# A cross-attention kernel on one core: the order of the first 60 microseconds and of the last ten

## The chip, the cores and the metric

The kernel runs on one core of a Trainium2 chip. The metric is the device time of one launch in microseconds (us). The time before is 1426.85 us, the median of three runs (1426.43 to 1427.44).

## The reference

64 batches, all in float32; x is 64x256x512, the context c is 64x256x384.

```python
text_p  = einsum('bld,dh->blh', H_l, W_text)  + b_text     # q, 512 wide
audio_p = einsum('bsd,dh->bsh', H_a, W_audio) + b_audio    # k and V, 512 wide
Q = layer_norm(text_p, g1, beta1)
K = layer_norm(audio_p, g2, beta2)
alpha = softmax(einsum('blh,bsh->bls', Q, K) * scale)
H_hyper = einsum('bls,bsh->blh', alpha, audio_p)
H_hyper = einsum('blh,hk->blk', H_hyper, W_out) + b_out
out = layer_norm(H_hyper + H_l, g_out, beta_out)
```

## The kernel before

All is in one function, `tile_xattn_kernel`, with the order of the instructions on every engine written out by hand: each engine runs its instructions in the order of the text, and waits at the first one whose inputs, or whose buffer, are not there yet. The same holds of the queue in which SyncE issues the DMAs.

A batch passes these stages. Its x and c are read as "squares" (`load_x`, `load_c`: four DMAs each, by L88), so that VectorE's transposes of 32x32 blocks (`turn_x`, `turn_c`, L91) give x and c with the channels on the partitions. TensorE multiplies them with the weights; from batch 1 on the two halves of each side are multiplied as seven products instead of eight (class `Blocks`). For these, GpSimd forms sums and differences of the blocks (`sum_x`, `sum_c`, `weight_sums`) and VectorE adds the products from PSUM to the rows that they belong to (`leave`, L483, seven instructions). ScalarE (ACT) takes the squares of the rows (`square`, L380); GpSimd makes the scales of them, (variance + eps) to the power -0.5 (L341, L343); ACT multiplies the rows by these (`normalise`, L408). The rows go to DRAM (`store`, L418) and come back as squares (`fetch`, L88), VectorE turns them (`turn`), ACT applies gamma and beta (`affine`, L446), and then come the scores (L511), maxima (L521), exponentials (L528), and the context (L577). Only batch 0 is different: its c and x come as rows and are transposed on TensorE (`RowTurn`), and its products are whole (`Projection.multiply`, L362), with their moments taken on VectorE.

The weights are centred over the hidden channels first (`means` on ACT, L275; `centre` on VectorE, L282), so that the mean of each later row is zero. W_audio times W_out is formed once (`turn_weights`, `fold_multiply`, `fold_evict`, L245 and L254), with its bias (`bias_parts`, L231 and L233; `fold_bias`), since alpha times V times W_out is alpha times c times that product. `keep_busy` multiplies a tile of ones, with no use of the result. `take_columns` transposes the vectors gamma, beta and b_audio on TensorE and copies them on ACT.

The first part, up to the loop, does all this for batch 0 and the projections of batch 1. Turn b of the loop, for b from 0 to 61, takes the scores of batch b, q and k of batch b + 2, the turn of the squares of batch b + 3, and the output of batch b - 1, among others. Before, the turns and sums of batch b + 3 stand right ahead of the maxima in every turn. After the loop a part written out by hand finishes the last batches: `last` is batch 61, `at` batch 62 and `end` batch 63. The very last rows are multiplied and settled in two halves (`multiply_halves`, `evict_halves`, `settle_halves`), each with a DMA of its own.

`shift` subtracts the mean and multiplies by g_out; `settle` multiplies by the row's scale, which comes from GpSimd (`scales`), and adds beta_out. PSUM has six banks for products and two for the rest; SBUF's work tiles have two buffers each, so a tile of batch b + 2 waits until that of batch b has been read.

Of the kernel before, what the change touches and what calls it, by code (L numbers as in the profile page):

```python
# [15 lines left out]
P = 128  # L16
# [6 lines left out]
def kernel(  # L23
# [82 lines left out]
    def load_squares(b):  # L106
        load_c(b)
        load_x(b)
# [23 lines left out]
    def row(v, name):  # L132
        t = const.tile([P, H], F32, tag=name, name=name)
        nc.sync.dma_start(t, v.rearrange("(o h) -> o h", o=1).broadcast_to([P, H]))
        return t
# [11 lines left out]
    def weight_chunks(t, w, lo, n, queues):  # L147
        v = w.rearrange("(q k i) h -> q i k h", q=NQ, i=SQ)
        for q in range(NQ):
            queues[q].dma_start(t[q * SQ : (q + 1) * SQ, lo : lo + n], v[q, :, lo : lo + n])  # L150

    nc.sync.dma_start(c_0[:, :1], c_rows[:, :1])
    weight_chunks(wa_sb, w_audio, 0, 1, [nc.scalar, nc.sync, nc.scalar, nc.sync])
    nc.scalar.dma_start(c_0[:, 1:], c_rows[:, 1:])
    weight_chunks(wa_sb, w_audio, 1, 2, [nc.sync] * NQ)
    for t in range(LT):
        nc.sync.dma_start(x_0[:, t, :], x_rows[:, t, :])
    weight_chunks(wt_sb, w_text, 0, 2, [nc.sync] * NQ)
# [30 lines left out]
    def keep_busy(n):  # L189

        ps = p_pj.tile([P, P], F32, tag="pj", name="ps_ones")
        for _ in range(n):
            nc.tensor.matmul(ps, lhsT=ones, rhs=ones, start=True, stop=True)  # L193
# [59 lines left out]
    def fold_evict(a):  # L253
        nc.scalar.copy(wao_sb[:, a, :], ps_wao.pop(a))  # L254
# [9 lines left out]
    def moments(mv, src, t):  # L264

        st = small.tile([P, 6], F32, tag="st", name="st")
        nc.vector.bn_stats(st, src)
        nc.vector.bn_aggr(mv[:, t, :], st)

    def means(rows, n, name):  # L270

        m = const.tile([P, n], F32, tag=name, name=name)
        for k in range(n):
            junk = work.tile([P, H], F32, tag="junk", name="junk")
            nc.scalar.activation(  # L275
                junk, rows[:, k, :], AF.Identity, scale=-1.0 / H, accum_out=m[:, k : k + 1]
            )
        return m

    def centre(rows, m, n):  # L280
        for k in range(n):
            nc.vector.tensor_scalar(rows[:, k, :], rows[:, k, :], m[:, k : k + 1], None, ALU.add)  # L282
# [31 lines left out]
    def sum_c(cT, tag="csum"):  # L314

        part = lambda i, j: cT[:, j, bass.ts(i, P)]
        s = work.tile([P, 5, P], F32, tag=tag, name=tag)
        add = nc.gpsimd.tensor_tensor
        add(s[:, 0], part(1, 0), part(1, 1), ALU.add)
        add(s[:, 1], s[:, 0], part(0, 0), ALU.subtract)  # L320
        add(s[:, 2:4], cT[:, 0:3:2, :P], cT[:, 0:3:2, P:], ALU.subtract)
        add(s[:, 4], part(0, 1), s[:, 1], ALU.subtract)
        return {
            1: [part(0, 0)], 2: [part(0, 1), part(0, 2)], 4: [part(1, 1), part(1, 2)],
            5: [s[:, 0], part(1, 2)], 6: [s[:, 1]], 7: [s[:, 2]], 3: [s[:, 4], s[:, 3]],
        }
# [172 lines left out]
    class Attention:  # L499
# [143 lines left out]
            self.r = getattr(self, "r", {})  # L643
            self.r.update({lo + t: r for t, r in enumerate(rstd_of(self.mv[:, lo : lo + n, 1], n))})

        def moments(self):
            self.mv = small.tile([P, LT, 2], F32, tag="mvy", name="mvy")
            for t in range(LT):
                moments(self.mv, self.y[:, t, :], t)
            self.scales()  # L650

        def multiply_halves(self, t):
            self.ps_h = []
# [67 lines left out]
    def turn_c(b):  # L721
        cT = work.tile([P, AC, S], F32, tag="cT", name=f"cT_{b}")
        turn(cT, blocks[b][0], AC)
        return cT

    def add_bias(b):
        xb = rows[b][0]
        for t in range(LT):
            nc.gpsimd.tensor_tensor(xb[:, t, :], xb[:, t, :], bao_sb, ALU.add)  # L729
# [6 lines left out]
    x_turn = RowTurn(x_0, DC, "xT")  # L736
    k[0] = Projection("k", 0, c_turn.T, wa_sb, ba_sb, AC, ST)
    q[0] = Projection("q", 0, x_turn.T, wt_sb, bt_sb, DC, LT)
    keep_busy(12)
    c_turn.tile(0)  # L740
    keep_busy(8)
    k[0].multiply(0, [0])
    c_turn.tile(1)
    k[0].multiply(1, [0])
    k[0].multiply(0, [1, 2])
    k[0].multiply(1, [1, 2])
    mean_wa = means(wa_sb, AC, "mwa")
    war = []
    for a in range(AC):
        war.append(work.tile([P, HC, P], F32, tag="e" if a == 0 else "eT", name=f"war_{a}"))  # L750
        arrange(war[a], wa_sb[:, a, :], HC, nc.gpsimd.tensor_copy)
    x_turn.tile(0)
    x_turn.tile(1)
    centre(wa_sb, mean_wa, AC)
    wa_blocks = weights_of_three(wa_sb, "wasum")
    for chunks in ([0, 1], [2, 3]):
# [1 line left out]
            q[0].multiply(t, chunks)  # L758
    ba_row = ba_sb.rearrange("p (o h) -> p o h", o=1)
    bt_row = bt_sb.rearrange("p (o h) -> p o h", o=1)  # L760
    k[0].evict(0)
    k[0].evict(1)
    k[0].scales()
    mean_ba = means(ba_row, 1, "mba")
    mean_wt = means(wt_sb, DC, "mwt")
    cT[1] = turn_c(1)
    cs = {1: sum_c(cT[1])}
    centre(ba_row, mean_ba, 1)
    k[0].normalise()
    k[0].store()  # L770
    load_vectors()
    k[0].fetch()
    centre(wt_sb, mean_wt, DC)
    waT = turn_weights()
    wt_blocks = weight_sums(wt_sb, DC // 2, "wtsum")
    q[0].evict(0)
    q[0].evict(1)
# [2 lines left out]
    centre(bt_row, mean_bt, 1)  # L780
    q[0].normalise()
    q[0].store()
    bo_sb = row(b_out, "bo")
    q[0].fetch()
    load_squares(2)
    xT[1] = turn_x(1)
    k[1] = Blocks("k", 1, cs.pop(1), wa_blocks, ba_sb)
    k[1].products(1, 2)
# [6 lines left out]
    k[1].leave(3)  # L795
    k[1].leave(7)
    k[1].products(4)
    g1_sb, be1_sb, g2_sb, be2_sb, bac_sb = take_columns()
    k[1].leave(4)
    k[1].square()  # L800
    k[1].scales()
    xs = {1: sum_x(xT[1])}

    for v in (g2_sb, be2_sb):
        nc.vector.tensor_scalar(v, v, scale, None, ALU.mult)
    k[0].turn()
    k[1].normalise()
    k[1].store()
    k[1].fetch()
    k[0].affine(g2_sb, be2_sb)  # L810
    load_squares(3)
    fold_multiply(0)
    fold_evict(0)
    fold_multiply(1)
    fold_evict(1)
    part = bias_parts()
    xT[2] = turn_x(2)
    xs[2] = sum_x(xT[2])
    cT[2] = turn_c(2)
    cs[2] = sum_c(cT[2])  # L820
    q[0].turn()
    q[0].affine(g1_sb, be1_sb)
    q[1] = Blocks("q", 1, xs.pop(1), wt_blocks, bt_sb)
    q[1].products(1, 2)
    q[1].leave(1)
    q[1].products(6, 5)
    q[1].leave(6)
    q[1].leave(2)
# [5 lines left out]
    q[1].leave(4)  # L834
    q[1].square()
    q[1].scales()
    fold_multiply(2)
    fold_evict(2)
    bao_sb = fold_bias(part)
# [8 lines left out]
    for b in range(B - 2):  # L848
        three = b + 3 < B
        at = Attention(b)  # L850
        at.scores()
        if done:
            done.o.leave(3)
            done.o.leave(7)
            done.o.leave(4)
            done.add_x()
        if last:
            last.turn_e()
        if three:
            xT[b + 3] = turn_x(b + 3)  # L860
            xs[b + 3] = sum_x(xT.pop(b + 3))
            cT[b + 3] = turn_c(b + 3)
            cs[b + 3] = sum_c(cT.pop(b + 3))
        at.maxima()
        at.exponentials()
        q2 = q[b + 2] = Blocks("q", b + 2, xs.pop(b + 2), wt_blocks, bt_sb)
        q2.products(1, 2)
        q2.leave(1)
        at.reciprocals()
        at.divide_e()  # L870
        if b:
            q[b + 1].fetch()
            k[b + 1].fetch()
        at.store_e()
        if b + 4 < B:
            load_squares(b + 4)
        at.fetch_e()
        rows[b + 1] = load_rows(b + 1)
        if done:
            done.statistics()  # L880
        q2.products(6, 5)
        q2.leave(6)
        q2.leave(2)
        q2.leave(5)
        q2.products(7, 3)
        q2.leave(3)
        q2.leave(7)
        q2.products(4)
        q2.leave(4)
        q2.square()  # L890
        q2.scales()
        q[b + 1].turn()
        if done:
            done.shift(0)
            done.shift(1)
        if last:
            last.context()
        q[b + 1].affine(g1_sb, be1_sb)
        k[b + 1].turn()
        k[b + 1].affine(g2_sb, be2_sb)  # L900
        if done:
            done.settle(0)
            done.settle(1)
            done.store()
        q2.normalise()
        q2.store()
        if last:
            last.start_products()
        k2 = k[b + 2] = Blocks("k", b + 2, cs.pop(b + 2), wa_blocks, ba_sb)
        k2.products(1, 2)  # L910
        k2.leave(1)
        k2.products(6, 5)
        k2.leave(6)
        k2.leave(2)
        k2.leave(5)
        k2.products(7, 3)
        k2.leave(3)
        k2.leave(7)
        k2.products(4)
        k2.leave(4)  # L920
        k2.square()
        k2.scales()
        k2.normalise()
        k2.store()
        if last:
            last.o.products(1, 2)
            last.o.leave(1)
            last.o.products(6, 5)
            last.o.leave(6)
            last.o.leave(2)  # L930
            last.o.leave(5)
            last.o.products(7, 3)
            last.o.products(4)
        done, last = last, at
# [41 lines left out]
    at.context()  # L976
    done.settle(1)
    done.store()
    last.moments()
    end = Attention(B - 1)  # L980
    end.scores(end=True)
    at.start_output()
    at.multiply(0)
    last.shift(0)
    end.maxima()
    end.exponentials()
    last.shift(1)
    last.settle(0)
    last.settle(1)
# [18 lines left out]
    end.scales(0, 1)  # L1008
    end.multiply_halves(1)
    end.shift(0)  # L1010
    end.settle(0)
    end.store(0, 1)
    end.evict_halves(1)
    end.scales(1, 1)
    end.shift(1)
    end.settle_halves(1)


# [30 lines left out]
```

## Time and profile before

| | us |
|---|---|
| median of three runs | 1426.85 |
| the profiled execution, own time | 1425.56 |
| its span, first to last instruction | 1423.7 |
| TensorE busy | 1407.9 |
| VectorE busy | 1272.0 |
| ACT busy | 932.1 |
| GpSimd busy | 874.3 |

The busy shares of the whole span come first, and the chain of work that ended last, followed back from the last instruction. In a timeline each line has the start and the length of a group of instructions, the engine (PE is TensorE, DVE is VectorE, POOL is GpSimd, SPq is SyncE's DMA queue), the line of the kernel, the operation with its tiles, and how many there are; in brackets stands how long the engine had stood idle before it, and what ended that. Starts are microseconds from the first instruction. A float32 matmul shows as two records. Where a group shows no bracket, the engine went straight on.

The granted clock of TensorE is 0.998 over the span. Its activity is dense in all but the first and the last of 40 slices.

### The profile page before, as it was taken

Reading aid. Unit: us, or ns where it says so; the run is one execution under the profiler, and the core shown is the slowest. Engines: PE = TensorE matmul, PEld = TensorE weight load, DVE = VectorE, ACT = ScalarE, POOL = GpSimd, SP = SyncE. Lnnn points to the kernel's source line nnn. Section 1 sums busy time; section 2 is a strip of 40 time slices with the busy share of each in tenths; the row PEclk is TensorE's granted clock in tenths of the full one; section 3 lists DMA queues with packets and bytes.
Section 4 is the critical chain, followed back from the end, with each engine's and each line's share of the span. In section 5 each row is a group of like instructions: output and inputs, shape, how many; then the busy total and the mean of one; then the engine's idle time right before and its main releaser. Section 6 shows DMA issues by size and latency. Waiting matters only on the chain.

```text
span 1423.7 us, 23376 instructions
## 1 busy us (share of the span) xinstructions
PE 1407.9 (99%) x6465; PEld 1223.3 (86%) x6465; DVE 1272.0 (89%) x2134; ACT 932.1 (65%) x2293; POOL 874.3 (61%) x1295
## 2 busy tenths in 40 slices
PE   9899999999999999999999999999999999999997
PEld 6688888888888888888888888888888888888885
DVE  5689999999999999999999999999999999999987
ACT  4566676676766766766766766767767667667662
POOL 5556566566576566666666665665755665666644
PEclk9999999999999999999999999999999999999999
DMA  8798888787888878878878887887888788888763
GB/s 196 190 259 239 239 229 236 226 231 238 234 226 236 241 216 240 246 210 238 238 225 233 234 230 227 235 235 228 227 240 236 219 241 243 215 238 244 206 195 105
DMA packets 450582, 322.61 MB, mean 227 GB/s; under 512 B 154900, under 2 KB 382996, under 8 KB 450452
## 3 DMA queue, kind: packets, MB, share of 16 engines
q1 hardware_dynamic: 450212, 320.78, 80.0%
q8 instruction: 53, 0.87, 0.3%
q14 instruction: 77, 0.63, 0.1%
q10 hardware_dynamic: 240, 0.33, 0.1%
HBM read 204.09 MB, written 116.92 MB: 225 GB/s over the span
## 4 chain that ended last, share of the span: by engine, by line
PE 93%; DVE 2%; POOL 2%; DMA 1%; issue 1%; ACT 1%; SPq 0%; DVEq 0%; POOLq 0%
PE ps_q L472 26%; PE ps_y L472 20%; PE ps_k L472 20%; PE ps_sc L511 15%; PE ps_z L577 11%; PE ps_q L362 1%; PE ps_ones L193 0%; SPq L88 0%; DMA qd<-qr 0%; POOL yr L593 0%; PE ps_k L362 0%; POOL x L729 0%; DVE qr L483 0%; POOL ve L341 0%; POOL rstd L343 0%
## 5 line engine op out<-in xcount | busy, mean ns | idle before, releaser
L511 PE MATMUL ps_sc<-kT,qT 128*128 128x256 f32 x1024 | 232.0, 380 | 3.9 <-ACT kT L446 3.2
L341 POOL TENSOR_SCALAR ve<-var 128x2 f32<-128x2 f32 x126 | 42.9, 341 | 307.2 <-ACT junk L380 307.2
L528 ACT ACTIVATE e<-ps_sc,nmx 128x256 f32<-128x256 f32 x128 | 59.4, 469 | 250.1 <-DVE nmx L521 250.1
L511 PEld LDWEIGHTS ps_sc<-kT,qT 128*128 128x128 f32 x1024 | 193.9, 190 | 32.4 <-ACT kT L446 4.2
L483 DVE TENSOR_TENSOR qr<-ps_q,qr 128x512 f32<-128x512 f32 x378 | 188.3, 512 | 33.9 <-PE ps_q L472 18.2
L483 DVE TENSOR_TENSOR kr<-ps_k,kr 128x512 f32<-128x512 f32 x378 | 188.4, 512 | 24.7 <-PE ps_y L472 0.5
L483 DVE TENSOR_TENSOR yr<-ps_y,yr 128x512 f32<-128x512 f32 x372 | 185.3, 512 | 24.1 <-DVE yr L483 0.9
L593 POOL TENSOR_TENSOR yr<-yr,x 128x512 f32<-128x512 f32 x124 | 156.9, 1275 | 58.1 <-DVE yr L483 58.1
L577 PE MATMUL ps_z<-eT,c 128*128 128x256 f32 x768 | 176.5, 379 | 0.1
L472 PE MATMUL ps_q<-wtsum,xsum 128*128 128x256 f32 x756 | 173.4, 379 | 0.0
L343 POOL TENSOR_TENSOR rstd<-ve,nhalf 128x2 f32<-128x2 f32 (+1 forms) x194 | 158.2, 816 | 16.1
L472 PE MATMUL ps_k<-wa,cT 128*128 128x256 f32 x630 | 166.8, 379 | 0.0
L472 PE MATMUL ps_y<-wao,zT 128*128 128x256 f32 x620 | 164.2, 379 | 0.0
L577 PEld LDWEIGHTS ps_z<-eT,c 128*128 128x128 f32 x768 | 145.8, 190 | 20.7 <-ACT e L528 0.5
L472 PEld LDWEIGHTS ps_q<-wtsum,xsum 128*128 128x128 f32 x756 | 143.6, 190 | 19.5
L380 ACT ACTIVATE junk<-kr 128x512 f32<-128x512 f32 x126 | 79.4, 630 | 97.0 <-DVE kr L483 97.0
L446 ACT ACTIVATE qT<-qT,columns 128x256 f32<-128x256 f32 x256 | 133.0, 592 | 11.5 <-DVE qT L91 11.5
L472 PEld LDWEIGHTS ps_k<-wa,cT 128*128 128x128 f32 x630 | 119.6, 190 | 16.2
L446 ACT ACTIVATE kT<-kT,columns 128x256 f32<-128x256 f32 x256 | 132.3, 590 | 0.7 <-DVE kT L91 0.5
L472 PEld LDWEIGHTS ps_y<-wao,zT 128*128 128x128 f32 x620 | 117.7, 190 | 16.0
L408 ACT ACTIVATE kr<-kr,rstd 128x512 f32<-128x512 f32 x126 | 84.1, 714 | 71.0 <-POOL rstd L343 71.0
L701 DVE SCALAR_TENSOR_TENSOR yr<-yr,rstd,beo 128x512 f32<-128x512 f32 x124 | 126.8, 1060 | 0.0
(150 smaller groups left out, 2950.9 us busy)
## 6 DMA issues: line engine op xcount, KB each, us to landing
kd<-kr SPq DMA_DIRECT2D x64, 512.0 KB, 3.1
kq<-kd SPq DMA_DIRECT2D x256, 128.0 KB, 3.4
qd<-qr SPq DMA_DIRECT2D x64, 512.0 KB, 4.9
qq<-qd SPq DMA_DIRECT2D x256, 128.0 KB, 3.3
xq<-in_x_dram SPq DMA_DIRECT2D x252, 128.0 KB, 2.9
x<-in_x_dram SPq DMA_DIRECT2D x63, 512.0 KB, 4.1
out_dram<-yr SPq DMA_DIRECT2D x62, 512.0 KB, 4.9
cq<-in_ctx_dram SPq DMA_DIRECT2D x252, 96.0 KB, 2.5
```

The lines of the kernel that those rows point to most:

```text
L341: nc.gpsimd.tensor_scalar(ve, var, EPS, None, ALU.add)
L343: nc.gpsimd.tensor_tensor(r, ve, nhalf[:, :n], ALU.pow)
L380: nc.scalar.activation(junk, self.rows[:, t, :], AF.Square, scale=1.0 / math.sqrt(H), accum_out=self.var[:, t : t + 1],)
L408: nc.scalar.mul(row, row, self.r[t])
L446: nc.scalar.activation(self.T[:, k, :], self.T[:, k, :], AF.Identity, bias=bet[:, k : k + 1], scale=gam[:, k : k + 1],)
L472: nc.tensor.matmul(bank[:, j, :], lhsT=side, rhs=w, start=(i == 0), stop=(i == len(pairs) - 1))
L483: add = lambda o, i0, i1: nc.vector.tensor_tensor(o, i0, i1, ALU.add)
L511: nc.tensor.matmul(self.sc[:, t, :], lhsT=self.qT[:, k, bass.ts(t, P)], rhs=self.kT[:, k, :], start=(k == 0), stop=(k == HC - 1),)
L528: nc.scalar.activation(self.e[:, t, :], self.sc[:, t, :], AF.Exp, bias=self.nmx[:, t : t + 1], accum_out=self.den[:, t : t + 1],)
L577: nc.tensor.matmul(ps[:, j, :], lhsT=self.c_sb[:, s, bass.ts(lo + j, P)], rhs=self.eT[:, s, :], start=(s == 0), stop=(s == ST - 1),)
L593: nc.gpsimd.tensor_tensor(self.y[:, t, :], self.y[:, t, :], self.xb[:, t, :], ALU.add)
L701: nc.vector.scalar_tensor_tensor(self.y[:, t, :], self.y[:, t, :], self.r[t], beo_sb, ALU.mult, ALU.add)
```

## The change

At the start: fewer multiplies of ones; the second tile of batch 0's c is issued by SyncE, behind W_audio, instead of ACT; the products of batch 0's k run by tile, not by chunk; ACT takes the means of W_audio after its copies of x; k[0]'s first eviction stands ahead of centring W_audio; k[0]'s scales stand behind the sums of c[1]; centring W_text and turning W_audio stand ahead of normalising k[0]. The squares of batches 2 and 3 are issued one input at a time, behind a fetch or a store, instead of both together behind the fetch. The first two folds stand ahead of the columns and their evictions behind normalising k[1]. The turn of k[0] follows, q[0]'s turn and affine stand behind the first leave of q[1], and batch 2's turns and sums behind q[1]'s scales. In the first turn of the loop batch 3's turns and sums stand behind q[2]'s scales instead of ahead of the maxima; all later turns are as before.

At the end: `moments` can take one tile; the second moments and the first shift of batch 61 stand behind batch 63's maxima and exponentials; the settle and store of batch 63's first rows stand behind the evictions and shift of its last rows.

No computation is added or left out but the multiplies of ones. The diff, with the loop's context cut:

```diff
     weight_chunks(wa_sb, w_audio, 0, 1, [nc.scalar, nc.sync, nc.scalar, nc.sync])
-    nc.scalar.dma_start(c_0[:, 1:], c_rows[:, 1:])
     weight_chunks(wa_sb, w_audio, 1, 2, [nc.sync] * NQ)
+    nc.sync.dma_start(c_0[:, 1:], c_rows[:, 1:])
...
-        def moments(self):
-            self.mv = small.tile([P, LT, 2], F32, tag="mvy", name="mvy")
-            for t in range(LT):
+        def moments(self, tiles=range(LT)):
+            if 0 in tiles:
+                self.mv = small.tile([P, LT, 2], F32, tag="mvy", name="mvy")
+            for t in tiles:
                 moments(self.mv, self.y[:, t, :], t)
-            self.scales()
+            if LT - 1 in tiles:
+                self.scales()
...
+    def turn_next(b):
+        xT[b] = turn_x(b)
+        xs[b] = sum_x(xT.pop(b))
+        cT[b] = turn_c(b)
+        cs[b] = sum_c(cT.pop(b))
...
-    keep_busy(12)
+    keep_busy(6)
     c_turn.tile(0)
-    keep_busy(8)
-    k[0].multiply(0, [0])
+    keep_busy(2)
+    k[0].multiply(0, range(AC))
     c_turn.tile(1)
-    k[0].multiply(1, [0])
-    k[0].multiply(0, [1, 2])
-    k[0].multiply(1, [1, 2])
-    mean_wa = means(wa_sb, AC, "mwa")
+    k[0].multiply(1, range(AC))
     war = []
...
     x_turn.tile(0)
     x_turn.tile(1)
+    mean_wa = means(wa_sb, AC, "mwa")
+    k[0].evict(0)
     centre(wa_sb, mean_wa, AC)
...
-    k[0].evict(0)
     k[0].evict(1)
-    k[0].scales()
     mean_ba = means(ba_row, 1, "mba")
     mean_wt = means(wt_sb, DC, "mwt")
     cT[1] = turn_c(1)
     cs = {1: sum_c(cT[1])}
+    k[0].scales()
     centre(ba_row, mean_ba, 1)
+    centre(wt_sb, mean_wt, DC)
+    waT = turn_weights()
     k[0].normalise()
     k[0].store()
     load_vectors()
     k[0].fetch()
-    centre(wt_sb, mean_wt, DC)
-    waT = turn_weights()
+    load_c(2)
     wt_blocks = weight_sums(wt_sb, DC // 2, "wtsum")
...
     q[0].store()
-    bo_sb = row(b_out, "bo")
+    load_x(2)
     q[0].fetch()
-    load_squares(2)
     xT[1] = turn_x(1)
...
     k[1].products(4)
-    g1_sb, be1_sb, g2_sb, be2_sb, bac_sb = take_columns()
     k[1].leave(4)
     k[1].square()
     k[1].scales()
     xs = {1: sum_x(xT[1])}
+    fold_multiply(0)
+    fold_multiply(1)
+    g1_sb, be1_sb, g2_sb, be2_sb, bac_sb = take_columns()
...
-    k[0].turn()
     k[1].normalise()
     k[1].store()
+    bo_sb = row(b_out, "bo")
+    load_c(3)
     k[1].fetch()
+    load_x(3)
+    fold_evict(0)
+    fold_evict(1)
+    k[0].turn()
     k[0].affine(g2_sb, be2_sb)
-    load_squares(3)
-    fold_multiply(0)
-    fold_evict(0)
-    fold_multiply(1)
-    fold_evict(1)
     part = bias_parts()
-    xT[2] = turn_x(2)
-    xs[2] = sum_x(xT[2])
-    cT[2] = turn_c(2)
-    cs[2] = sum_c(cT[2])
-    q[0].turn()
-    q[0].affine(g1_sb, be1_sb)
     q[1] = Blocks("q", 1, xs.pop(1), wt_blocks, bt_sb)
     q[1].products(1, 2)
     q[1].leave(1)
+    q[0].turn()
+    q[0].affine(g1_sb, be1_sb)
     q[1].products(6, 5)
...
     q[1].scales()
+    xT[2] = turn_x(2)
+    xs[2] = sum_x(xT[2])
+    cT[2] = turn_c(2)
+    cs[2] = sum_c(cT[2])
     fold_multiply(2)
...
-        if three:
-            xT[b + 3] = turn_x(b + 3)
-            xs[b + 3] = sum_x(xT.pop(b + 3))
-            cT[b + 3] = turn_c(b + 3)
-            cs[b + 3] = sum_c(cT.pop(b + 3))
+        if three and b:
+            turn_next(b + 3)
         at.maxima()
         at.exponentials()
...
         q2.scales()
+        if three and not b:
+            turn_next(b + 3)
         q[b + 1].turn()
...
-    last.moments()
+    last.moments([0])
     end = Attention(B - 1)
     end.scores(end=True)
     at.start_output()
     at.multiply(0)
-    last.shift(0)
     end.maxima()
     end.exponentials()
+    last.moments([1])
+    last.shift(0)
     last.shift(1)
...
     end.shift(0)
-    end.settle(0)
-    end.store(0, 1)
     end.evict_halves(1)
     end.scales(1, 1)
     end.shift(1)
+    end.settle(0)
+    end.store(0, 1)
     end.settle_halves(1)
```

## The prediction, made before the changed kernel was run

> **What bounds the kernel now.** I read the page's busy shares and chain first, then the timeline of each engine over the first 95 us and the last 30 us, since those are the only stretches that the change edits. The page:
>
> ```profile
> PE 1407.9 (99%) x6465; PEld 1223.3 (86%) x6465; DVE 1272.0 (89%) x2134; ACT 932.1 (65%) x2293; POOL 874.3 (61%) x1295
> ...
> PE 93%; DVE 2%; POOL 2%; DMA 1%; issue 1%; ACT 1%; SPq 0%; DVEq 0%; POOLq 0%
> ```
>
> TensorE is the bound, and 93% of the chain is its matmuls. Its timeline shows where it is not dense:
>
> ```profile
> 1.53 5.16 PE L193 MATMUL ps_ones<-ones 128*128 128x128 f32 x24 [1.53 <-POOL ones L122]
> 6.86 1.95 PE L193 MATMUL ps_ones<-ones 128*128 128x128 f32 x16
> 10.56 4.56 PE L362 MATMUL ps_k<-wa,cT 128*128 128x512 f32 x10 [0.57 <-ACT cT L210]
> 47.95 3.90 PE L511 MATMUL ps_sc<-kT,qT 128*128 128x256 f32 x16 [0.69 <-ACT qT L446]
> 65.88 3.90 PE L511 MATMUL ps_sc<-kT,qT 128*128 128x256 f32 x16 [3.24 <-ACT kT L446]
> 87.75 3.62 PE L511 MATMUL ps_sc<-kT,qT 128*128 128x256 f32 x16
> ```
>
> Ahead of 10.56 it mostly multiplies ones; at 65.88 (the scores of batch 1) it stands 3.24 us. From there it repeats with no gap, 21.58 us a batch (87.75 to 109.33 and on). So the start is worth what it moves that 65.88; the end is a chain of its own. Why the scores stand, on VectorE and in SyncE's DMA queue:
>
> ```profile
> 44.03 1.25 DVE L91 STREAM_TRANSPOSE xT<-xq 128x1024 f32<-128x1024 f32 x1 [6.11 <-DMA xq<-in_x_dram]
> 45.20 0.93 DVE L91 STREAM_TRANSPOSE cT<-cq 128x768 f32<-128x768 f32 x1
> 46.06 1.20 DVE L91 STREAM_TRANSPOSE qT<-qq 128x1024 f32<-128x1024 f32 x1
> 47.18 0.65 DVE L483 TENSOR_TENSOR qr<-ps_q,bt 128x512 f32<-128x512 f32 x1
> 61.98 1.25 DVE L91 STREAM_TRANSPOSE qT<-qq 128x1024 f32<-128x1024 f32 x1 [1.47 <-DMA qq<-qd]
> ```
>
> ```profile
> 35.45 2.04 SPq L88 DMA_DIRECT2D qq<-qd x4
> 37.53 2.01 SPq L88 DMA_DIRECT2D cq<-in_ctx_dram x4
> 39.58 1.93 SPq L88 DMA_DIRECT2D xq<-in_x_dram x4
> ```
>
> TensorE had q[1]'s first products done at 38.5, but VectorE takes them only at 47.18: it stands 6.11 us for batch 2's squares, which SyncE issues behind qq, and then turns them. The rest of the leaves end at 51.2; square, scale, store and fetch of q[1] end at 61.98, then come the turn and the affine, and the scores at 65.88.
>
> **The change part by part: the first 66 us.** I put the new order of each engine on the old durations.
>
> *Fill-in and first products.* 12 of 20 ones-multiplies go (24 of 40 records). c's second tile moves from ACT's to SyncE's queue, behind 512 KB of w_audio: there 704 KB (256 KB records between the waits at 5.17 and 8.17) took 3.0 us, 235 GB/s, so w_audio lands 0.8 us earlier (7.4) and c's tile about 8.2; x's issues slip by one issue, 0.4, hidden by a queue that is 4.2 behind. TensorE: 12 records at 0.216 from 1.53 end at 4.1; c's first copy ends at 4.4; transposes and four more records to about 5.9; first chunk 5.9 to 6.8 (0.87 each), the others 7.4 to 9.15; second tile's transposes to 9.5, ACT copy 0.48, three products 10.05 to 12.65. Then x's transposes begin, 14.96 before: 2.3 earlier. w_text's first half (2.2 MB cumulative at 235 GB/s from 2 us, so 11.5[...]) is there for q at 13.9. q ends at 21.0 instead of 23.37.
>
> [...] The trace: the ones take 0.216 a record until 5.85, 0.12 after; 4.3 us of activity bring the full rate. [...] The new order leaves a hole of 0.3 us at 4.1. If the hole doesn't matter, nothing is lost; if the 4.3 us start again at 4.45, full rate comes at 8.8 and k's first products take 5.9 to 10.0, 0.85 later. I take the first ([...]the old 0.57 hole at 10.0 cooled nothing) and keep 0.85 for the range.
>
> *GpSimd.* The means of w_audio now follow ACT's copies of x (means 14.3 to 16.1); k's first eviction runs before centring, and w_audio is centred at 16.7 (16.0 before). Second eviction and statistics 1.6, turn of c[1] 0.95: 19.2. On GpSimd the sums of c (2.2) now stand ahead of k's scales (2.0): 23.5 for k's scales, 21.4 before. Weight sums (5.6) and q's scales (1.5) give 30.6, as before (30.7): centring w_text and the weight transposes ahead of k's normalising gain nothing there. ACT: q normalised at 32.1, squares of k[1] 33.7, GpSimd scales 34.7, xsum's first two of x[1] at 36.5 to 37.0.
>
> *TensorE on.* Weight transposes 1.66, k[1]'s products 4.75, two folds 6.9 and the columns' transpose 0.1: 21.0 to 34.4. q[1]'s first pair ends at 36.15; the next pair needs xsum: a new wait of 0.3 to 0.9, 0.6 taken. q[1] ends 41.1, third fold and bias 45.4, scores(0) 45.4 (47.95 before), q[2] 48.85 to 54.9, k[2] to 59.65 (62.64 before).
>
> *VectorE and its waits.* The columns' transpose now lies behind the folds: VectorE is done with k[1]'s leaves at 32.0 and stands to 34.8 for ACT's copy; queued behind are the two column scalings, k[0]'s turn, part and q[1]'s leaves. That costs nothing, since part (3.5) ends at 39.8, and q[1] waits for q[0]'s turn anyway. ACT's fold evictions after k[1]'s normalising (37.1) free banks needed at 41.1.
>
> *SyncE.* K's store waits for ACT: 25.1 (22.61). kq is issued 29.3 to 31.1, load_c(2) 31.1 to 33.1, qd 33.1 (32.27, so the store loses 0.8), load_x(2) to 35.4, qd lands at 36.5, qq to 38.4 and lands near 41.0. So load_c(2) and load_x(2), eight issues at 0.5, lie in two waits for stores; kd[1] goes at 38.4 instead of 41.62; bo, load_c(3), kq[1] and load_x(3) end at 45.8. q[0]'s turn is at 41.0 to 42.2, its affine to 44.3: 1.1 before the scores need it. q[1]'s other leaves end at 45.4 (51.2). Square and scales to 47.0, normalised 48.4, stored 48.5, fetch from 51.8, landed by 56.3.
>
> *Turns.* Batch 2's turns (2.1) lie at 45.4 to 47.5, sums on GpSimd at 47.0 to 52.1, q[2] needs the first two at 50.6. Batch 3's turns and sums, which stood ahead of the maxima at 53.40, now follow q[2]'s leaves: these end with TensorE's last product, 55.6. Then turns 2.1 to 57.7, q[1]'s turn 1.25, k[1]'s turn beside ACT; ACT's q affine 2.06 from 59.1, first k column 0.58: scores(1) at 61.7. TensorE was free at 59.65, so a wait of 2.1 stays and is now set by VectorE. Gain: 65.88 - 61.7 = 4.2. Batch 3's sums (done at 62.5) are needed at 65.2: hidden.
>
> **The end.**
>
> ```profile
> 1414.43 0.75 DVE L696 SCALAR_TENSOR_TENSOR y<-y,mvy,go 128x512 f32<-128x512 f32 x1
> 1415.94 0.75 DVE L701 SCALAR_TENSOR_TENSOR y<-y,rstd,beo 128x512 f32<-128x512 f32 x1 [0.75 <-POOL rstd L343]
> 1420.18 0.88 DVE L684 SCALAR_TENSOR_TENSOR y<-y,rstd,beo 128x256 f32<-128x256 f32 x2 [0.76 <-POOL rstd L343]
> ```
>
> VectorE is the chain here and stands twice for GpSimd's scale. The change moves the first settle (0.67 of step) behind the last shift, into the second wait: the halves follow at 1415.1 (their matmuls end at 1415.1), so 0.76 + 0.67 = 1.4 goes; the last scale then stays 1.55 behind the last moments, as before. The store of the first 256 KB moves to 1418.7, half a microsecond ahead of the halves: the trace moves 256 KB in about 1.0 (1417.4 to 1418.4), so contention costs 0 to 0.3; 0.1 taken. Maxima ahead of the second moments fill a wait of 0.31, but the scale then comes 0.1 late: 0.1 gained; TensorE's 0.48 wait there isn't on the chain. End: 1.4.
>
> **Sum.** 4.2 + 1.4 = 5.6. The profiled execution, span 1423.7 and own time 1425.56, becomes 1418.1 and 1420.0. It lies 1.3 under the median 1426.85 of three; so the median becomes 1421.3.
>
> **Rivals.** *The start gives part:* full rate late (0.85), the w_audio tile no earlier (0.8), xsum's wait 0.9 instead of 0.6: 2.0 less, 1423.3. For it: GpSimd has no slack from 19 to 37. *The start gives almost nothing* because VectorE's new order only trades waits (columns, then qq, then batch 3's turns ahead of q[1]'s): scores(1) within 1 us of now and the end's 1.4: 1425. Against it: each of these ends before the next thing it feeds. *The early qq turns into a block, slower:* q[0]'s turn now stands ahead of six leaves of q[1]. With qq landing at L, q[1]'s turn is ready at L + 15.3 and scores(1) at L + 19.3. It decides from L = 42.4 and loses all above 46.6 (48.0 with the end); at L = 51, as if kq, cq, xq and qd ran one after the other at the 4 us each that a landing took, scores(1) come at 70.3 and the kernel at 1429.9. Against it: in the old trace qq was there by 46.06 at the latest, issued 35.45, and its landing took 2.9.
>
> **Numbers.** As worked out 65%; partly 14%; start lost 13%; slower 8%. The range 1419.5 to 1424.3 holds the first two: 5.6 less 2.6 at most, or with TensorE free at 59.65 and no wait 2 more. 0.2% is 2.85 us, about what a measurement of this kernel can tell from no change: faster (under 1424.0) 0.77, same 0.15, slower 0.08.
>
> **What would show it.** Right: first k products near 6, x's transposes near 12.7, no wait on ACT qT at scores(0), q[1]'s leaves done near 45.4, scores(1) near 61.7 with a wait of about 2 on ACT kT behind turns of batch 3, then 21.58 a batch; the last settle beside GpSimd's scale. Wrong: matmuls at half rate past 6 us; a DMA named as what ended VectorE's idle before qT at 41 or later; any new TensorE gap behind 66 us.

## The result, and the profile after

| | before | after |
|---|---|---|
| median of six runs each, us | 1426.64 (1425.84 to 1427.44) | 1421.76 (1420.36 to 1422.65) |
| profiled execution, own time | 1425.56 | 1420.47 |
| its span | 1423.7 | 1418.7 |
| start of the scores of batch 1 | 65.88 | 61.47 |
| from the scores of batch 63 to the end | 26.8 | 26.1 |

The ratio is 0.9964, with an interval of 0.9951 to 0.9977: 4.9 us faster in the medians, 5.1 in the profiled executions. The last two rows split the 5.1: 4.41 from the start (the scores of batch 63 move by just as much, 1396.95 to 1392.54, so nothing is won or lost in between) and 0.7 from the end. Five of the 14 profiles lose 1.6 to 2.7 us to a fall of TensorE's granted clock, told of below; single spans are compared at the starts of instructions ahead of such a fall.

The page of the changed kernel, its busy shares and its chain:

```profile
PE 1405.0 (99%) x6441; PEld 1220.9 (86%) x6441; DVE 1273.3 (90%) x2134; ACT 931.8 (66%) x2293; POOL 875.2 (62%) x1295
...
PE 94%; DMA 2%; DVE 1%; POOL 1%; SPq 1%; issue 1%; ACT 0%; POOLq 0%; DVEq 0%; ACTq 0%
```

TensorE is the bound as before; its 24 records less are those of ones. Its timeline:

```profile
1.53 2.93 PE L193 MATMUL ps_ones<-ones 128*128 128x128 f32 x12 [1.53 <-POOL ones L122]
...
5.80 3.34 PE L362 MATMUL ps_k<-wa,cT 128*128 128x512 f32 x6
...
12.71 1.04 PE L209 MATMUL ps_rows<-ident,xTr 128*128 128x128 f32 x8
...
45.16 3.62 PE L511 MATMUL ps_sc<-kT,qT 128*128 128x256 f32 x16
...
61.47 3.90 PE L511 MATMUL ps_sc<-kT,qT 128*128 128x256 f32 x16 [1.90 <-ACT kT L446]
...
83.34 3.62 PE L511 MATMUL ps_sc<-kT,qT 128*128 128x256 f32 x16
```

The first products stand at 5.80, the transposes of x 2.2 us earlier than before, and the wait for q's turn at the first scores (0.69) is gone. But the first of the six records was not at full rate (1142 ns, where the last take 592). L362 in parts of this stretch (shortest, median and longest record in ns, then the first and last start):

```profile
L362 PE MATMUL ps_k<-wa,cT x1: 1142/1142/1142, 5.8 to 5.8; 128*128 128x512 f32 x1
...
  DMA wa<-in_L_xattn_W_audio_dram: 0.8, 1
...
L362 PE MATMUL ps_k<-wa,cT x3: 592/592/592, 7.7 to 8.5; 128*128 128x512 f32 x3
```

The second record starts 0.93 behind the first, where the last ones follow each other by 0.43. The loss cost nothing: the weights of the third record could be loaded only when w_audio's next part had landed, at 7.06 (the 0.8 in the middle).

At 61.47 a wait of 1.90 is left of 3.24. Its row names the same releaser as before, but the cause is another, as VectorE shows:

```profile
41.24 1.25 DVE L91 STREAM_TRANSPOSE qT<-qq 128x1024 f32<-128x1024 f32 x1 [0.56 <-DMA qq<-qd]
42.41 3.23 DVE L483 TENSOR_TENSOR qr<-ps_q,qr 128x512 f32<-128x512 f32 x6
45.55 1.24 DVE L91 STREAM_TRANSPOSE xT<-xq 128x1024 f32<-128x1024 f32 x1
...
55.59 1.24 DVE L91 STREAM_TRANSPOSE xT<-xq 128x1024 f32<-128x1024 f32 x1
56.75 0.94 DVE L91 STREAM_TRANSPOSE cT<-cq 128x768 f32<-128x768 f32 x1
57.61 1.20 DVE L91 STREAM_TRANSPOSE qT<-qq 128x1024 f32<-128x1024 f32 x1
```

The 6.11 us for batch 2's squares are gone: q[1]'s leaves end at 45.6 instead of 51.2. The last three rows have no bracket: VectorE goes straight through batch 3's turns into q[1]'s turn, so that turn no longer waits for a DMA but for two turns ahead of it. SyncE's queue:

```profile
33.03 2.45 SPq L88 DMA_DIRECT2D xq<-in_x_dram  x4
35.85 2.29 SPq L88 DMA_DIRECT2D qq<-qd  x4
...
48.89 0.38 SPq L418 DMA_DIRECT2D qd<-qr  x1
51.71 1.79 SPq L88 DMA_DIRECT2D qq<-qd  x4
```

Batch 2's x is now issued ahead of q[0]'s fetch, in the time in which q[0]'s store lands. At the end VectorE has these waits:

```profile
1399.60 1.42 DVE L703 SCALAR_TENSOR_TENSOR yr<-yr,rstd,beo 128x512 f32<-128x512 f32 x2 [0.60 <-POOL rstd L343]
...
1413.23 0.75 DVE L698 SCALAR_TENSOR_TENSOR y<-y,mvy,go 128x512 f32<-128x512 f32 x1
1413.90 0.74 DVE L703 SCALAR_TENSOR_TENSOR y<-y,rstd,beo 128x512 f32<-128x512 f32 x1
1415.11 0.88 DVE L686 SCALAR_TENSOR_TENSOR y<-y,rstd,beo 128x256 f32<-128x256 f32 x2 [0.46 <-POOL rstd L343]
```

The settle at 1413.90 now lies in the wait for the last scale, and one of the two waits shown of before is gone. But 0.46 of the other stays, and the first row has a wait of 0.60 that was not there.

### The profile page after: what moved, and what is told of

Same layout as the page of the kernel before. It is cut to its first block, busy times and chain, and to the rows that moved or that the text cites. A ratio compares the mean times of both kernels' runs of the same rounds, so it can differ in the third digit from the quotient of the medians.

```text
span 1418.7 us, 23330 instructions
## 1 busy us (share of the span) xinstructions
PE 1405.0 (99%) x6441; PEld 1220.9 (86%) x6441; DVE 1273.3 (90%) x2134; ACT 931.8 (66%) x2293; POOL 875.2 (62%) x1295
## 4 chain that ended last, share of the span: by engine, by line
PE 94%; DMA 2%; DVE 1%; POOL 1%; SPq 1%; issue 1%; ACT 0%; POOLq 0%; DVEq 0%; ACTq 0%
PE ps_q L472 26%; PE ps_y L472 21%; PE ps_k L472 20%; PE ps_sc L511 15%; PE ps_z L577 11%; DMA qq<-qd 0%; DMA xq<-in_x_dram 0%; DMA qd<-qr 0%; DMA wt<-in_L_xattn_W_text_dram 0%; SPq L150 0%; DMA bt<-in_L_xattn_b_text_dram 0%; POOL rstd L343 0%; POOL ve L341 0%; DVE qr L483 0%; DVE st L267 0%
```

## The experiments

The theory: the start gives 4.4 us, through two things that both have to be there (earlier first products, and squares issued in SyncE's waits), and batch 3's turns now set what is left; the end gives 0.7 (0.6 in the expectations, from rounded spans), since the maxima edit costs something. The rivals are named with each group.

One execution starts up to 1.2 us later than another before any edit acts: with the new first products x's transposes start between 12.69 (e3) and 13.92 (e10). So beside the start of the scores of batch 1 stands their distance from the scores of batch 0. It is 17.93 us before and 16.31 in after, e2 and e3; the other 2.79 of the 4.41 are there at the scores of batch 0 already.

**One part alone.** `e1_tail_only` has the start of before and the end of after, `e2_start_only` the reverse. If the end gave the predicted 1.4 and the start less, these two would show it.

> Only the edits at the end, on the start of before. Theory (the start carries 4.4 us, the end the rest): scores of batch 1 stay at 65.9 us, the span comes 0.6 under 1423.7. Rival (the end gives the 1.4 us that the prediction had, and the start less than its 4.4): 1.4 under.

> Only the edits at the start, with the end of before. Theory: scores of batch 1 near 61.5 us, from there to the last instruction 1357.8 as before, so a span near 1419.3, 0.6 above the changed kernel. Rival (the end gives 1.4): 1420.1.

Measured: e1 1426.52 (1425.38 to 1428.34), ratio 1.0 (0.9991 to 1.0009); e2 1422.24 (1421.35 to 1424.36), ratio 0.997 (0.996 to 0.9981). From the scores of batch 63 to the end e1 takes 26.1 and e2 26.9; e2's scores of batch 1 start at 61.64. e1's own profile is 2.8 longer than that of before, since it began 0.7 late and its clock fell. So the start carries nearly all, and the end alone can't be told from nothing in the medians; its 0.7 is read from single executions.

**The maxima edit undone**, the settle's move kept (this base serves e4, e9 and e12 too):

```diff
-    last.moments([0])
+    last.moments()
...
+    last.shift(0)
     end.maxima()
     end.exponentials()
-    last.moments([1])
-    last.shift(0)
     last.shift(1)
```

> The changed kernel, with the second moments and the first shift of batch 61 ahead of batch 63's maxima again; the last settle stays behind the last shift. Theory (GpSimd's power takes 1.07 instead of 0.71 because it lies beside two shifts, so the earlier maxima cost 0.47): the power is back at 0.71, the wait of 0.60 ahead of L703 goes, the span is 0.5 shorter. Rival (the earlier maxima fill a wait of 0.31, as predicted): 0.1 longer.

Measured: 1421.09 (1419.66 to 1421.97), ratio 0.9961 (0.9947 to 0.9975). The medians can't tell it from after; the profiled span is 0.8 shorter, at the same start (61.51). GpSimd's power that makes the scale, in after:

```profile
1398.50 1.07 POOL L343 TENSOR_TENSOR rstd<-ve,nhalf 128x2 f32<-128x2 f32 x1
...
1414.14 0.93 POOL L343 TENSOR_TENSOR rstd<-ve,nhalf 128x1 f32<-128x1 f32 x1
```

and in e3, with the row of VectorE that needs it:

```profile
1397.82 0.71 POOL L343 TENSOR_TENSOR rstd<-ve,nhalf 128x2 f32<-128x2 f32 x1
```

```profile
1398.84 1.41 DVE L703 SCALAR_TENSOR_TENSOR yr<-yr,rstd,beo 128x512 f32<-128x512 f32 x2
```

In e3 the power takes 0.71 and the settles follow with no wait. In after, the moments end 0.7 later behind the scores, the power starts beside the second shift and takes 1.07, and the settles wait 0.60. From the scores to the first eviction behind them (L632) after takes 8.39, e3 7.59 and e2, with the same order here as e3, 8.0: the edit costs 0.4 to 0.8. The settle's move can be read behind that point: from that eviction to the end e2 takes 18.9 and e3 17.7 (before 18.9, after 17.7), so it gives 1.1 to 1.2.

**Which edit of the start carries it.** Each of these is after with one edit undone. In e5 batch 2's turns and sums stand ahead of q[1]'s products again; in e6 the squares are issued both together behind a fetch; in e7 batch 3's turns stand ahead of the maxima in the first turn of the loop too; in e8 the first products, the ones and c's second tile are as before.

```diff
 e5   part = bias_parts()
+     xT[2] = turn_x(2)     # with sum_x(2), turn_c(2), sum_c(2)
 e6   k[0].fetch()
-     load_c(2)
-     load_x(2)
      q[0].fetch()
+     load_squares(2)       # batch 3 likewise, behind k[1].fetch()
 e7   if three and b:   ->   if three:
 e8   keep_busy(6), (2)  ->  keep_busy(12), (8); k[0] by chunk; c_0's tile on ACT
```

> The changed kernel with batch 2's turns and sums back ahead of q[1]'s first leave and q[0]'s turn. Theory (the place of these turns on VectorE cost the old kernel most, through the wait for the squares; the squares now come early): no wait, q[1]'s leaves end 1.7 to 2.1 later (47.3 to 47.7), its squares come back at 57.5 to 58, scores of batch 1 within 0.8 of 61.5. Rival (VectorE's place matters in itself): scores of batch 1 at 63.5 or later.

> The changed kernel with the DMA issues of batches 2 and 3 together again behind the fetches of q[0] and k[1]. Theory (VectorE's order carries the start, the issue order little, since batch 2's squares are needed only at 45.5): scores of batch 1 within 0.8 us of 61.5. Rival (the issues in the queue's waits carry it): 63 us or more, with a DMA named ahead of a turn on VectorE.

> The changed kernel with batch 3's turns and sums ahead of batch 0's maxima, as before. Theory (behind q[2]'s leaves these turns stand on the path for 2.1 us; ahead of the maxima they would lie beside TensorE's q[2]): scores of batch 1 at 59.6 to 60, 1.5 to 1.9 better than the changed kernel. Rival (they stand for their squares, the maxima and the exponentials come late, and all behind them): scores of batch 1 at 62 or later.

> The changed kernel with 20 multiplies of ones, c's second tile in ACT's queue and k[0]'s products by chunk, as before. Theory (TensorE is dense from there to q[2]'s end, so the 2.3 us of the first products go through to the scores of batch 1): x's transposes at 15.0, scores of batch 1 near 63.5. Rival (GpSimd's sums bound the start, 19 to 37 us): scores of batch 1 within 0.5 of 61.5.

| | median (range), us | ratio (interval) | scores of batch 1 | from those of batch 0 | wait there |
|---|---|---|---|---|---|
| e5 | 1422.34 (1420.95 to 1423.5) | 0.9967 (0.9956 to 0.9978) | 61.91 | 16.30 | 1.90 |
| e6 | 1425.94 (1424.28 to 1426.61) | 0.9991 (0.9983 to 1.0) | 64.95 | 19.51 | 5.11 |
| e7 | 1421.14 (1419.91 to 1422.29) | 0.9962 (0.9947 to 0.9977) | 60.91 | 15.62 | 1.22 |
| e8 | 1424.36 (1421.78 to 1424.79) | 0.998 (0.9974 to 0.9987) | 63.84 | 16.31 | 1.90 |

e5's place makes no difference that can be told: with the squares issued early, VectorE doesn't wait for them there either. e8 agrees with the theory: its x transposes start at 15.10, and the scores 2.4 later than in after, with the same distance. In e7 the change's own edit turns out to cost 0.7 at the scores, where 1.5 to 1.9 was expected: ahead of the maxima the turns lie in time that VectorE has to spare (it waits 1.56 there for its buffer to be read), and only part of their cost comes ahead of q[1]'s turn. The 0.7 is kept: from the scores of batch 1 to those of batch 2 e7 takes 21.87, as after does.

My expectation for e6 failed, and the rival held: the places in SyncE's queue carry 3.2 us (19.51 for 16.31; its execution also began 0.3 late). The queue in e6:

```profile
47.58 1.93 SPq L88 DMA_DIRECT2D cq<-in_ctx_dram  x4
49.56 1.92 SPq L88 DMA_DIRECT2D xq<-in_x_dram  x4
51.99 0.38 SPq L418 DMA_DIRECT2D qd<-qr  x1
55.56 2.98 SPq L88 DMA_DIRECT2D qq<-qd  x4
```

and what it makes of VectorE and TensorE:

```profile
61.05 1.25 DVE L91 STREAM_TRANSPOSE qT<-qq 128x1024 f32<-128x1024 f32 x1 [3.09 <-DMA qq<-qd]
```

```profile
64.95 6.33 PE L511 MATMUL ps_sc<-kT,qT 128*128 128x256 f32 x16 [5.11 <-ACT kT L446]
```

q[1]'s leaves end at 45.4 in e6 as well, but its store stands behind eight issues of batch 3's squares until 51.99; in after it goes at 48.89. From store to fetch it takes 3.57 instead of 2.82, and the rows are there at 61.05; in after they were there near 55.9 (an estimate from e4, where VectorE has just waited for them at 55.91) and 1.7 of that lead was spent behind batch 3's turns, so 3.4 is left. So the order that brings q[1]'s rows early is worth little unless the queue is free when they come: with the old queue order it makes this stretch longer than before (19.51 against 17.93). The rest of e6's loss is a fall of the clock: 16 products take 6.33 instead of 3.90. The new places of the folds, the columns and the turns of k[0] and q[0], and the three parts of e8, were not undone one by one.

**The wait that is left.** Rivals: the 1.90 is VectorE's, set by batch 3's turns, or something stands right behind it. e4 is e3 with these turns moved behind k[1]'s turn; e9 is e3 with x's turn behind the exponentials and c's behind `divide_e`; e12 is e4 with batch 4's x issued behind e's fetch in the first turn.

```diff
 e4      q2.scales()
-        if three and not b:
-            turn_next(b + 3)
         q[b + 1].turn()
...
         k[b + 1].turn()
+        if three and not b:
+            turn_next(b + 3)
 e12     at.fetch_e()
+        if not b:
+            load_x(b + 4)
```

> As the run before, and in the first turn of the loop batch 3's turns and sums stand behind the turns of q[1] and k[1], not ahead of them. Theory (VectorE's 2.1 us of batch 3's turns set the last wait of TensorE, 1.9 us): the scores of batch 1 start at 59.6, right behind k[2]'s products, and the span is 1.9 shorter than in the run before. Rival (q[1]'s DMA sets it): qq lands at 55.6 or later and the wait stays above 1 us.

> As the run with the old maxima order (e3), with batch 3's turn of x behind batch 0's maxima, its turn of c behind the reciprocals, and its sums behind q[2]'s scales: in two waits of VectorE of about 1 us each ahead of q[2]'s leaves. Theory (these turns were on the path only for their place): q[2]'s leaves still end near 55.7, scores of batch 1 at 59.8 with 0.2 of wait, and no new wait behind it as the 0.6 that e4 had ahead of ps_y; the span is 0.8 shorter than e4's 1417.2. Rival (VectorE is full, so each microsecond put there pushes q[2]'s leaves): scores of batch 1 at 60.8 or later.

> As e4, and in the first turn of the loop batch 4's squares of x are issued behind the fetch of e, not ahead of it. Theory (with the wait of 1.9 gone, e's squares come last: VectorE stands 1.09 for them at 65.4, and TensorE 0.57 ahead of ps_y for what follows): e's squares are there when k[2]'s leaves end at 64.3, the wait ahead of ps_y goes, the scores of batch 2 come 21.9 behind those of batch 1 (22.7 in e4), the span is 0.6 shorter than e4's 1417.2. Rival (the four issues only change places): VectorE then stands as long for batch 4's x, the wait ahead of ps_y stays.

e4 is 1419.44 (1418.99 to 1420.31), ratio 0.995 (0.9935 to 0.9965): the fastest of all, 2.3 under after in the medians. Its profiled span is 0.7 under that of e3, its base, where 1.9 was expected. Its TensorE:

```profile
59.81 3.90 PE L511 MATMUL ps_sc<-kT,qT 128*128 128x256 f32 x16 [0.19 <-ACT kT L446]
...
80.26 0.67 PE L472 MATMUL ps_y<-waosum,zsum 128*128 128x256 f32 x2 [0.57 <-DVE kr L483]
...
82.49 3.62 PE L511 MATMUL ps_sc<-kT,qT 128*128 128x256 f32 x16
```

The wait falls to 0.19, so it was VectorE's, set by the turns. But the scores of batch 2 move from 83.34 to 82.49 only: 0.8 of the 1.7 is given back in a new wait 20 us later. VectorE's turn of the squares of e starts at 65.36, after a stand of 1.09: only 0.24 earlier than in after, while TensorE is 1.7 earlier, and everything of that turn of the loop is queued behind it. SyncE's queue in e4 shows why e is late:

```profile
54.68 0.38 SPq L546 DMA_DIRECT2D ed<-e  x1
55.10 2.10 SPq L88 DMA_DIRECT2D cq<-in_ctx_dram  x4
57.24 4.04 SPq L88 DMA_DIRECT2D xq<-in_x_dram  x4
61.32 1.93 SPq L88 DMA_DIRECT2D eq<-ed  x4
```

The fetch of e stands behind four issues of batch 4's x that take 4.04 us together (the other sets of four squares in this run take 1.8 to 3.1; why these take longer isn't shown). e9 and e12 do no better:

```profile
67.50 0.71 DVE L91 STREAM_TRANSPOSE eT<-eq 128x512 f32<-128x512 f32 x1 [4.28 <-DMA eq<-ed]
```

(e9; 1420.25, 1419.07 to 1421.63, ratio 0.9956, 0.9944 to 0.9969), and

```profile
67.03 1.25 DVE L91 STREAM_TRANSPOSE xT<-xq 128x1024 f32<-128x1024 f32 x1 [2.14 <-DMA xq<-in_x_dram]
```

(e12; 1421.5, 1420.85 to 1423.8, ratio 0.9966, 0.9952 to 0.998). In e12 e no longer waits, but x, issued behind it, does, and the later wait of TensorE grows from 0.57 to 2.05; behind it e12's clock fell in the profiled execution. In e9 the wait at the scores falls to 0.33, so the two gaps do hold batch 3's turns. But x's issues end at 63.58 instead of 61.28, e comes 2.1 later than in e4, and TensorE's later wait is 1.67; 0.8 of the 2.1 is this execution's late start, and the rest is issues of c and x that took 7.7 together instead of 6.1, so e9's order itself isn't shown to be worse. Of the two transfers that want one place in the queue, the second made TensorE late in e4 and in e12; an order that serves both wasn't found.

**The ones and the clock.** e11 is after with one multiply of ones in place of each of the two groups (`keep_busy(6)` and `(2)` both become `(1)`); e10 is after with ten more multiplies of ones ahead of the scores of batch 1, to fill the 1.90.

```diff
 e10     at = Attention(b)
+        if b == 1:
+            keep_busy(10)
         at.scores()
```

> The changed kernel with one multiply of ones instead of six and one instead of two. Theory (the rate rises only after some 4.3 us of activity): k[0]'s first products at half rate until about 8.6, x's transposes at 13.8 instead of 12.7, the median 1.1 up. Rival (the ones aren't needed, the data of w_audio set the start): x's transposes at 12.7 to 12.9, no change.

> The changed kernel with ten multiplies of ones [...]ahead of the scores of batch 1, in the wait of 1.9. Theory (in some executions the granted clock falls to 0.5 in or behind this wait, which costs 1.6 to 2.7 us and makes the spread of the runs): the scores start at 61.5 as before, no execution falls, the times lie within 1 us and their median near 1420.5. Rival (the spread has its cause in the first 8 us, where the clock rises): the spread of 2.3 us and the median 1421.8 stay.

e11 is 1422.64 (1422.17 to 1423.66), ratio 0.9971 (0.996 to 0.9982):

```profile
1.53 0.79 PE L193 MATMUL ps_ones<-ones 128*128 128x128 f32 x2 [1.53 <-POOL ones L122]
4.30 0.90 PE L209 MATMUL ps_rows<-ident,cTr 128*128 128x128 f32 x3 [1.98 <-DVE cTr L184]
...
5.78 5.22 PE L362 MATMUL ps_k<-wa,cT 128*128 128x512 f32 x6
...
14.57 1.04 PE L209 MATMUL ps_rows<-ident,xTr 128*128 128x128 f32 x8
```

With a hole of 1.98 the six products take 5.22 instead of 3.34, and x's transposes come 1.9 later than in after, where 1.1 was expected: the ones that are left are needed. The scores of batch 1 come 1.8 later too (63.31). e10 is 1421.21 (1420.41 to 1421.99), ratio 0.9962 (0.9948 to 0.9975), with a mean clock of 0.998 in every run, where three of after's six show 0.996 or 0.997. Its spread is 1.6 where after's is 2.3. That fits, but I had expected the times within 1 us, and half a microsecond between medians is within the intervals. In its profile the ones take 2.23, more than the wait that they fill. And TensorE stood 0.69 for c's second tile, so that x's transposes came 1.2 later than in after (13.92): part of the spread comes from the first 10 us and not from the clock, as the rival had it.

## Why the prediction was right

The prediction was 1421.3 and the median is 1421.76. Step by step:

- **First products.** Predicted near 5.9, x's transposes 12.65, q's end 21.0; measured 5.80, 12.71, 21.1. e8 prices this step at 2.4 of the scores' start, against 2.3 predicted for x's transposes. Of the clock, the prediction's reading did not hold: it had full rate from 5.85 on in the old trace, after 4.3 us of activity, and named half rate past 6 us as a sign of being wrong. The first clock record of a trace, which grants full rate, lies at 6.21 before (4.7 from the first ones) and only at 6.92 in after. The sign came true and cost nothing, since w_audio landed at 7.06; the prediction had that landing in its sum, but not as what would hide a late clock, so this was luck. The hole of 0.3 didn't come about, since the transposes follow the ones at 4.25 without a gap, so whether such a hole matters wasn't tested. With one of 1.98 (e11) L362's records take 1061 ns or more up to 10.2 and the last, from there, 794: full rate near 10.6, an estimate from the 592 of a record at full rate. That 4.3 us of activity bring it was the prediction's estimate from one trace; from the first ones to full rate it took 4.7 before, 5.4 in after and 9.1 in e11.
- **GpSimd.** k's scales end at 24.2 (23.5 predicted). The first three sums of x[1] took 0.73 each, not the 1.07 to 1.2 of the row before: VectorE scaled the columns and ran k[0]'s transposes beside them, and L233 (`part`) no longer. So q[1]'s products lost some 0.3 to them, not 0.6, and the scores of batch 0 came at 45.16, not 45.4.
- **VectorE and SyncE.** q[0]'s turn at 41.24 (41.0), q[1]'s leaves to 45.6 (45.4), store at 48.89 (48.5), fetch at 51.71 (51.8), batch 3's turns from 55.59 (55.6), q[1]'s turn at 57.61 (57.7), the scores at 61.47 (61.7) with a wait of 1.90 (2.1). That the wait is VectorE's is shown by e4; that the issues in the stores' waits are what lets the rest count, by e6.
- **Turns of batch 3.** That they lie ahead of q[1]'s turn was in the sum, but not that their old place would have been better; e7 shows 0.7 for it.
- **The end** was mis-sized: 0.7, not 1.4. The settle's move was put at 1.4 with "the last scale then stays 1.55 behind the last moments"; it lies 1.91 behind, because the power takes 0.93 beside the settle where it took 0.57 while VectorE stood idle. So the move gives 1.1. And the maxima edit, put at a gain of 0.1, costs 0.4 to 0.8: its power takes 0.36 longer in the same way, and the moments end later. No contention of the stores shows: the last instruction ends 2.7 behind the last settle before and after.
- **The sum.** 4.41 + 0.7 = 5.1 in the profiles, for 4.2 + 1.4 = 5.6 predicted: errors of +0.2 and -0.7, which partly cancel by luck. The ends of the range, 1419.5 and 1424.3, don't quite come out of its own terms (1421.3 less 2 and plus 2.6 give 1419.3 and 1423.9); that has no effect here.
- **The rivals.** Parts of the start that give less, a start lost in traded waits, and q[0]'s turn as a block did not occur: VectorE stood 0.56 for q[0]'s squares at 41.24, and the block would have begun at 42.4. So 1.2 us of margin were left. That row is another sign that the prediction had named as wrong, a DMA ending VectorE's idle before qT at 41 or later; it came true, and was too strict, since the sum itself bears such a wait up to 42.4. The third, a new gap of TensorE behind 66 us, did not come.

What the prediction didn't have is the clock fall of some runs; its size lies within the prediction's range.

## What to carry to other kernels

When rows come earlier than before, look at what is queued ahead of their store: an order on the engines pays only if the DMA queue's order follows it (3.2 us in e6), and a queue's waits for stores are the place for issues that nothing waits for yet. A step moved into a wait isn't free if the engine that is waited for gets slower beside it (the power, 0.93 for 0.57); take its length from a row that stands beside the same VectorE instruction, not from one beside an idle VectorE or another instruction. Removing one wait at the head of a repeating loop shows its worth only at the next repetition: read the same instruction one turn later. There e4, which took away 1.7, keeps 0.9, and e7, which took away 0.7, keeps it all. And compare distances inside one execution where executions start at different times.

## What the runs showed of the hardware

**The granted clock fell in or behind a wait, in some runs.** In e8's profile TensorE waits 1.90 us and goes on at 63.84. Its answer by stretches of 1 us (busy shares of PE, PEld, DVE, ACT and POOL, then the clock, the DMA share and GB/s):

```profile
63.00:64.00 1.00, 0.16 (x1) 0.17 (x2) 0.92 (x2) 1.00 (x3) 0.92 (x3) 1.00 1.11 312
64.00:65.00 1.00, 1.00 (x4) 0.66 (x5) 0.90 (x3) 1.00 (x3) 0.83 (x2) 0.76 0.90 195
65.00:66.00 1.00, 1.00 (x3) 0.78 (x3) 0.86 (x3) 1.00 (x3) 0.00 (x0) 0.50 0.73 198
66.00:67.00 1.00, 1.00 (x4) 0.79 (x3) 0.31 (x1) 1.00 (x4) 0.00 (x0) 0.50 0.64 147
67.00:68.00 1.00, 1.00 (x4) 0.82 (x3) 0.00 (x0) 0.71 (x4) 0.20 (x1) 0.53 0.81 123
68.00:69.00 1.00, 1.00 (x6) 0.87 (x6) 0.77 (x2) 0.16 (x1) 0.72 (x2) 1.00 0.78 127
```

The clock is at 0.50 for 3.4 us (64.5 to 67.9, an estimate from these means), and the 16 records take 5.47 instead of 3.90. The same happened with the wait of 1.90 in e5 (5.52), of 3.11 in e1 (6.57) and of 5.11 in e6 (6.33), for 3.4 us in e5 and 6.8 in e1 and e6, by the means of their stretches. Behind 2.05 in e12 the next groups start 1.7 later than at full rate, so there too it fell for some 3.4, an estimate. It did not fall behind 1.90 in the profiles of after, e2, e3 and e11, nor behind 3.24 in that of before (3.90 or 3.91 each). e8's runs fall into two groups, four at 1421.8 to 1422.2 and sixteen at 1423.8 to 1424.8; after's three runs at 0.998 take 1420.4 to 1421.3, and its three at 0.996 or 0.997 take 1422.2 to 1422.7. What sets off the fall isn't shown: with the same 1.90 it came in two profiles and stayed away in four. With the wait at 0.19 (e4) no run was above 1420.4.

**GpSimd took longer beside some instructions of VectorE.** The first sum of x[1], 1.21 before and 0.73 after, and what VectorE ran beside it:

```profile
35.01 1.21 POOL L304 TENSOR_TENSOR xsum<-xT 128x256 f32<-128x256 f32 x1
34.89 3.03 DVE L233 SCALAR_TENSOR_TENSOR part<-wo,columns,part 128x512 f32<-128x512 f32 x3
...
34.86 0.73 POOL L304 TENSOR_TENSOR xsum<-xT 128x256 f32<-128x256 f32 x1
34.92 0.76 DVE L813 TENSOR_SCALAR columns<-columns 128x4 f32<-128x4 f32 x2 [2.72 <-ACT columns L179]
35.60 1.29 DVE L439 STREAM_TRANSPOSE kT<-kq 128x512 f32<-128x512 f32 x2
```

The 128x1 power took 0.57 with VectorE idle and 0.93 beside a settle, the 128x2 one 1.07 where it started beside a shift and 0.71 where it started beside the maxima. Shifts, settles and L233 are all SCALAR_TENSOR_TENSOR; the other instructions of VectorE were not told apart.

**The time to full rate** differed from profile to profile. The first ones start at 1.53 or 1.54 in every one, and the first clock record, of full rate, lies at 6.21 before and 6.92 in after. From the lengths of the groups it came, as estimates, near 4.9 in e5 (the three transposes at 4.35 take 0.79; 0.90 in after ahead of full rate, 0.49 behind it), near 7.6 in e1 (the 16 records of ones at 7.45 take 2.03; 1.95 in e8 at full rate) and, with the hole of e11, near 10.6. Before, a record of ones took 0.21 up to then and 0.11 from then on. The clock column of the windows (as in the table above) shows 1.00 ahead of the first clock record, so there the rate must be read from the starts of the records.
